# Second attention: scores of one head on 32 rows of the array, and a chunk's turns made in a step of their own

## The chip, the core and the metric

The kernel runs on one core of a Trainium2 chip. The metric is the device time of one execution in microseconds; the runs shown are three, and their median counts. The core has engines that run side by side and each work off a queue of their own in order: PE (matrix products, from SBUF into PSUM), DVE, ACT and POOL (vector work; here only the first two are given PSUM tiles, and POOL also issues indirect DMAs) and SP, which here issues DMAs. The kernel deals PSUM out in banks of 512 float32 values per partition. An engine waits for another through semaphores. PE's rows come in two kinds: PEld loads the weights (the stationary operand), PE streams the moving operand past them. A float32 matmul shows as two loads and two streams. Matmuls whose operands lie in 32 of the 128 rows, or whose outputs lie in 32 of the 128 columns, use a part of the array (32*128 or 128*32 in the rows).

## The reference

Two transformer layers over 8 sequences of 512 tokens and 256 features. Each layer normalizes, then adds an attention and a mixture of experts. The change lies in the second layer's attention, a gated linear attention with 8 heads of 32 features, which the reference writes as a scan over time:

```python
def step(M, inp):
    q_t, k_t, v_t, f_t, g_t, o_t = inp
    M = M * f_t[..., None, None] + g_t[..., None, None] * scale * (k_t[..., :, None] * v_t[..., None, :])
    y_t = jnp.einsum('bhd,bhde->bhe', q_t, M) * o_t[..., None]
    return (M, y_t)
```

`q` and `k` are rotated projections, `f`, `g` and `o` sigmoid gates by head; the rows `y` are then multiplied by `Wout` and added to the input.

## The kernel before

The scan is done by chunks of 128 tokens, `NT` = 4 per sequence. Within a chunk the sum over earlier tokens is a matrix product with a decay: for each head the scores k·q (keys on the partitions, queries along the free dimension) are multiplied by exp of the summed logs of the forget gates between the two tokens. What comes from earlier chunks goes through a state `m`, 256 by 32 values kept as two block-diagonal 128 by 128 matrices (four heads each), with decayed queries `qw` and decayed keys `kw`.

`prep1` (from L1265) makes a sequence's operands: `s_proj` (projections `pa`, `pb`, L1296, the rotation on DVE, L1311 to L1320), `s_gates`, and `s_decays` (PSUM tile `dec`, from which ACT makes `ew` and `tot`).

`main1` in `attention1` (from L1384) works through the chunks with two kinds of steps.

- `s_scores(c)`: ACT writes `u`, eight 128 by 128 tiles, one per head: the triangle `inc` times the head's logs (L1416). PE turns the chunk's queries and keys (`qkT`, L1420), ACT copies them out (L1422). Then for each half `hf` of four heads: PE puts a large negative number above the diagonal (`mask_gt`, L1426) and adds the logs' sums (`gt` times `u`, L1433) into `d`; ACT takes the exponential into `de` (L1437); DVE spreads the turned queries over four block-masked copies `qb` (L1440), so that one product over all 128 rows gives four heads' scores `a` (L1447); DVE multiplies to `am` (L1448). `d` and `a` take turns in two PSUM buffers of one bank each (pool `a1da`).
- `s_chunk(c)`: `qw` on DVE (L1460), turned on PE (L1463), copied by ACT (`qwTs`, L1465). For each half: the state's product (L1468), then four matmuls, one per head, each into its own 32 output partitions (L1472), all into `y`. ACT copies `yTs` (L1480). `kw` on DVE (L1485), its product with `v` into `pm` (L1488), from which DVE updates `m` (L1499 to L1503). Last the output product `po` (L1510) and the addition to `x` (L1513).

Eight PSUM banks are shared out as `mm` 2 (pa, pb, po), `tr` 2 (qkT, qwT), `da` 2, `y` 1, `sm` 1 (pm and dec).

`interleave` alternates the steps of sequence b with the `prep1` steps of the next. After each step `move()` issues some of a list of other steps: in part "a" (sequences 0 to 3) the end of the norms, the second layer's routing and the 64 indirect DMAs by which POOL sends rows to the experts' order (L437); in part "b" (sequences 4 to 7) the fetching (SP) and adding (DVE, L476) of the experts' results and the storing of finished sequences. Their number per step follows from `n_steps`. Between "a" and "b" the experts of layer two run, with the `prep1` of sequence 4 among them. The order in which the code issues steps is a priority: a scheduler works out a fixed order for each engine's queue before the run, and in the trace the instructions of neighbouring steps are mixed.

Of the kernel before, what the change touches and what calls it, by code (L numbers as in the profile page):

```python
# [84 lines left out]
def tile_two_layers(  # L85
# [1179 lines left out]
    def prep1(b, ap, ps_mm, ps_sm, held1, places=None):  # L1265

        wide = {"tag": "mm", "n": S} if places else {"tag": "sm", "n": 256}
# [86 lines left out]
        def s_decays():  # L1354
            flat = lf.rearrange("p t h -> p (t h)")
            ps = ps_sm.tile([P, wide["n"]], F32, tag=wide["tag"], name=f"dec{b}")
            nc.tensor.matmul(ps[:, 0:32], inc, flat, start=True, stop=True)
            nc.tensor.matmul(ps[:, 32:64], gt, flat, start=True, stop=True)

            lfx = new("lfx", NT - 2, H1, HD1)  # L1360
            nc.scalar.copy(lfx, bc(lf[:, 1 : NT - 1], HD1))
            lfx = lfx.rearrange("p t h d -> p t (h d)")
            for c in range(1, NT - 1):
                for hf in range(2):
                    n = 64 + 2 * c + hf
                    nc.tensor.matmul(
                        ps[:, n : n + 1],
                        lfx[:, c - 1, hf * P : (hf + 1) * P],
                        one,
                        start=True,  # L1370
                        stop=True,
                    )
            nc.scalar.activation(
                ew.rearrange("p i t h -> p (i t h)"), ps[:, 0:64], AF.Exp
            )
            nc.scalar.activation(
                tot[:, 1 : NT - 1].rearrange("p t i -> p (t i)"),
                ps[:, 66 : 64 + 2 * (NT - 1)],
                AF.Exp,
            )  # L1380
# [3 lines left out]
    def attention1(blocks, part, also, done, held1):  # L1384
        with tc.tile_pool(name=f"a1{part}", bufs=2) as ap, tc.tile_pool(
            name=f"a1mm{part}", bufs=2, space=PSUM
        ) as ps_mm, tc.tile_pool(name=f"a1tr{part}", bufs=2, space=PSUM) as ps_tr, tc.tile_pool(
            name=f"a1da{part}", bufs=2, space=PSUM
        ) as ps_da, tc.tile_pool(name=f"a1y{part}", bufs=1, space=PSUM) as ps_y, tc.tile_pool(
            name=f"a1sm{part}", bufs=1, space=PSUM  # L1390
        ) as ps_sm:
            wout = second["wout"]
            moves = deque(also(ap, ps_mm))
            n_steps = len(blocks) * (3 * NT + 2)
# [8 lines left out]
            def main1(b):  # L1403
# [8 lines left out]
                def s_scores(c):  # L1412

                    u = ap.tile([P, H1, P], F32, tag="u", name=f"u{b}_{c}")
                    for h in range(H1):
                        nc.scalar.activation(u[:, h, :], inc, AF.Copy, scale=lf[:, c, h : h + 1])  # L1416
# [6 lines left out]
                    am = ap.tile([P, 2, 4, P], F32, tag="am", name=f"am{b}_{c}")  # L1423
                    for hf in range(2):
                        pd = ps_da.tile([P, 4, P], F32, tag="da", name=f"d{b}_{c}_{hf}")
                        nc.tensor.matmul(  # L1426
                            pd,
                            ident_h,
                            mask_gt.unsqueeze(1).to_broadcast([P, 4, P]),
                            start=True,  # L1430
                            stop=False,
                        )
                        nc.tensor.matmul(  # L1433
                            pd, gt, u[:, 4 * hf : 4 * hf + 4, :], start=False, stop=True
                        )
                        de = ap.tile([P, 4, P], F32, tag="de", name=f"de{b}_{c}_{hf}")
                        nc.scalar.activation(de, pd, AF.Exp)  # L1437

                        qb = ap.tile([P, 4, P], F32, tag="qb", name=f"qb{b}_{c}_{hf}")
                        nc.vector.tensor_tensor(  # L1440
                            qb,
                            qkT[:, hf, :].unsqueeze(1).to_broadcast([P, 4, P]),
                            blk.unsqueeze(2).to_broadcast([P, 4, P]),
                            ALU.mult,
                        )
                        pa = ps_da.tile([P, 4, P], F32, tag="da", name=f"a{b}_{c}_{hf}")
                        nc.tensor.matmul(pa, qkT[:, 2 + hf, :], qb, start=True, stop=True)  # L1447
                        nc.vector.tensor_mul(am[:, hf], pa, de)  # L1448
                    got[c] = am

                def s_chunk(c):
                    am = got.pop(c)

                    py = ps_y.tile([P, 2, P], F32, tag="y", name=f"y{b}_{c}")
                    if c:
                        pt = ps_tr.tile([P, 4, P], F32, tag="tr", name=f"qwT{b}_{c}")
                    if c:

                        qw = ap.tile([P, H1, HD1], F32, tag="qw", name=f"qw{b}_{c}")
                        nc.vector.tensor_tensor(qw, qk[c][:, :H1], per_head(ew[:, 0, c]), ALU.mult)  # L1460
                        flat = qw.rearrange("p h d -> p (h d)")
                        for hf in range(2):
                            nc.tensor.transpose(pt[:, hf, :], flat[:, hf * P : (hf + 1) * P], ident)  # L1463
                        qwT = ap.tile([P, 2, P], F32, tag="qwT", name=f"qwTs{b}_{c}")
                        nc.scalar.copy(qwT, pt[:, :2, :])  # L1465
                    for hf in range(2):
                        if c:
                            nc.tensor.matmul(  # L1468
                                py[:, hf, :], m[:, hf, :], qwT[:, hf, :], start=True, stop=False
                            )  # L1470
                        for h in range(4):
                            nc.tensor.matmul(  # L1472
                                py[32 * h : 32 * h + 32, hf, :],
                                v[:, c, 4 * hf + h, :],
                                am[:, hf, h, :],
                                start=(c == 0),
                                stop=True,
                            )
                    yT = ap.tile([P, KD, P], F32, tag="yT", name=f"yTs{b}_{c}")
                    nc.scalar.copy(yT, py)  # L1480

                    if c < NT - 1:

                        kw = ap.tile([P, H1, HD1], F32, tag="kw", name=f"kw{b}_{c}")
                        nc.vector.tensor_tensor(kw, qk[c][:, H1:], per_head(ew[:, 1, c]), ALU.mult)  # L1485
                        pm = ps_sm.tile([P, 256], F32, tag="sm", name=f"pm{b}_{c}")
                        for hf in range(2):
# [6 lines left out]
                            )  # L1494
                        for hf in range(2):
# [20 lines left out]
                for c in range(NT):  # L1516
                    steps.append(lambda c=c: s_scores(c))
                    if c:
                        steps.append(lambda c=c: s_chunk(c - 1))
# [3 lines left out]
            def prep(b):  # L1523
                return prep1(b, ap, ps_mm, ps_sm, held1)
# [69 lines left out]
    with tc.tile_pool(name="m1w", bufs=4) as wp, tc.tile_pool(  # L1594
# [8 lines left out]
            prep1(B // 2, None, ps_p, ps_p, ready, places_of_prep()),  # L1603
# [101 lines left out]
```

## Time and profile before

| | |
|---|---|
| median of three runs | 1971.99 us (1968.79 to 1974.9) |
| the profiled execution | 1983.88 us, of which the span shown is 1982.2 |
| PE busy | 1775.9 us, 90% of the span |
| PEld busy | 1248.7 us, 63% |
| DVE, ACT, POOL busy | 825.1, 765.9, 399.2 us |
| mean granted PE clock | 0.951 |

Times in the profile are microseconds from the span's start unless marked ns. Matmuls overlap and their ends are modelled, so that a busy PE isn't PE at its peak; how long a group of matmuls really takes is read from the start of its first to the start of what follows. In a timeline row stand start, length, engine, line, operation, output<-inputs by the names in the code, the part of the array in rows*columns, the moving operand's shape and the number of instructions merged; in brackets the engine's idle time before it and what ended it. "<-issue" is time in which the profile shows nothing that was waited for.

### The profile page before, as it was taken

How to read it: one execution, taken by the hardware profiler on the slowest of the kernel's cores; microseconds unless marked ns; L12 is line 12 of the kernel's file. 1: busy time of each engine (PE TensorE's matmuls, PEld its weight loads, DVE VectorE, ACT ScalarE, POOL GpSimd, SP SyncE). 2: the span in 40 equal slices, each digit the busy share in tenths (PEclk: the TensorE clock that was granted, in tenths of full speed). 3: DMA queues.
4: the chain of work that ended last, by engine and by line, in shares of the span. 5: the costliest groups of instructions: out<-in, count | busy, mean ns of one | idle time of the engine just before them, and what ended most of it. 6: DMA issues, size and time to landing. Idle time of an engine off the chain costs nothing. (4 is left out here: it accounts for less than half of the span.)

```text
span 1982.2 us, 28295 instructions
## 1 busy us (share of the span) xinstructions
PE 1775.9 (90%) x10680; PEld 1248.7 (63%) x10680; DVE 825.1 (42%) x1886; ACT 765.9 (39%) x1432; POOL 399.2 (20%) x457
## 2 busy tenths in 40 slices
PE   5876988999999999997688469999999999999998
PEld 3434655666666666764344235578888889886455
DVE  5453333434344434344667337641111111114865
ACT  2333334344434443434345135532323333335455
POOL 2024441212212122121130660011111111011000
PEclk9988999999999999998788779999999999999999
DMA  8713220656634354333321330086666867572500
GB/s 247 196 48 141 82 92 23 192 167 179 196 120 144 132 178 135 114 112 95 113 89 35 117 119 1 1 292 218 232 227 218 309 228 262 211 298 74 165 11 22
DMA packets 163688, 289.18 MB, mean 146 GB/s; under 512 B 63952, under 2 KB 134624, under 8 KB 152928
## 3 DMA queue, kind: packets, MB, share of 16 engines
q1 hardware_dynamic: 148432, 248.77, 38.6%
q0 software_dynamic: 13088, 36.07, 4.9%
q10 hardware_dynamic: 2032, 2.54, 0.4%
q8 instruction: 84, 1.38, 0.3%
q14 instruction: 52, 0.43, 0.1%
HBM read 206.78 MB, written 67.94 MB: 139 GB/s over the span
## 5 line engine op out<-in xcount | busy, mean ns | idle before, releaser
L659 PE MATMUL gup<-xgT,ew 128*128 128x256 f32 (+1 forms) x2080 | 379.3, 337 | 3.5 <-DMA ew<-in_dram 1.9
L692 PE MATMUL gdn<-ew,hgT 128*128 128x256 f32 x1640 | 372.4, 381 | 0.0
L659 PEld LDWEIGHTS gup<-xgT,ew 128*128 128x128 f32 x2080 | 333.5, 192 | 40.3 <-issue 4.5
L692 PEld LDWEIGHTS gdn<-ew,hgT 128*128 128x128 f32 x1640 | 307.7, 190 | 48.6 <-issue 9.1
L969 DVE TENSOR_REDUCE mx<-sc 128x4 f32<-128x2048 f32 (+1 forms) x124 | 184.0, 1484 | 274.8 <-ACT pt L997 254.7
L997 ACT ACTIVATE pt<-sc 128x2048 f32<-128x2048 f32 (+3 forms) x128 | 158.3, 1237 | 238.1 <-PE sc L966 130.0
L719 POOL DMA_INDIRECT zd<-yo,row x144 | 140.1, 973 | 468.3 <-DVE yo L710 403.3
L670 ACT ACTIVATE hgT<-gup,ew 128x256 f32<-128x256 f32 (+1 forms) x376 | 133.1, 424 | 209.0 <-issue 123.2
L999 POOL TENSOR_SCALAR_AFFINE_SELECT pt<-pt 128x512 f32<-128x512 f32 x128 | 81.7, 638 | 650.1 <-ACT pt L997 648.6
L991 PE MATMUL sc<-qsh,k 32*128 32x512 f32 (+3 forms) x1024 | 114.1, 493 | 54.9 <-DVE mx L969 51.3
L710 DVE SCALAR_TENSOR_TENSOR yo<-ew,way,yo 128x256 f32<-128x256 f32 x72 | 31.7, 481 | 300.9 <-ACT yo L708 300.9
L437 POOL DMA_INDIRECT xd<-xr,pos x128 | 125.8, 983 | 61.0 <-issue 50.1
L1019 PE MATMUL av<-pt,vaug 128*32 128x512 f32 (+3 forms) x1024 | 88.6, 478 | 31.4 <-POOL pt L999 30.6
L991 PEld LDWEIGHTS sc<-qsh,k 32*128 32x128 f32 x1024 | 43.4, 187 | 113.7 <-DVE mx L969 83.8
L997 ACT ACT_TABLE_LOAD x42 | 53.9, 1283 | 158.2 <-PE sc L991 128.6
L964 PE MATMUL sc<-k,q 32*128 32x512 f32 (+1 forms) x992 | 108.1, 468 | 3.8 <-DMA k<-raw 3.8
L1019 PEld LDWEIGHTS av<-pt,vaug 128*32 128x32 f32 x1024 | 31.9, 118 | 83.1 <-issue 41.2
L1447 PE MATMUL a<-qb,qkTs 128*128 128x512 f32 x128 | 70.9, 637 | 11.9 <-DVE am L1448 9.3
L1028 DVE STREAM_TRANSPOSE ou<-av 128x512 f32<-128x512 f32 x32 | 22.9, 716 | 135.2 <-PE av L1019 119.8
L708 ACT ACTIVATE yo<-gdn,way 128x256 f32<-128x256 f32 x72 | 30.2, 473 | 125.8 <-PE gdn L692 125.7
L1433 PE MATMUL d<-u,cs 128*128 128x512 f32 x128 | 70.3, 633 | 3.9 <-ACT u L1416 3.9
L1416 ACT ACTIVATE u<-cs,lf 128x128 f32<-128x128 f32 x224 | 72.2, 394 | 0.0
(270 smaller groups left out, 2366.5 us busy)
## 6 DMA issues: line engine op xcount, KB each, us to landing
ew<-in_dram SPq DMA_DIRECT2D x47, 2180.0 KB
ew<-in_dram SPq DMA_DIRECT2D x36, 1024.0 KB
xd<-zero SPq DMA_DIRECT2D x12, 1572.0 KB
z<-zd SPq DMA_DIRECT2D x32, 512.0 KB
xnT<-in_dram SPq DMA_DIRECT2D x22, 512.0 KB
xg<-xd SPq DMA_DIRECT2D x36, 262.0 KB
xg<-xd SPq DMA_DIRECT2D x144, 64.0 KB
xn_d<-l_xn SPq DMA_DIRECT2D x16, 512.0 KB
```

What stands on the lines that cost most here:

```text
L437: i = nc.gpsimd.indirect_dma_start(out=self.xd, out_offset=bass.IndirectOffsetOnAxis(ap=self.pos[k][:, at : at + 1], axis=0), in_=held[b][ ...
L659: nc.tensor.matmul(ps[:, j, at : at + m], wu[u][:, k, f * P : (f + 1) * P], x, start=(k == 0), stop=(k == KD - 1),)
L670: nc.scalar.activation(ht[:, f, at : at + m], ps[:, j, at : at + m], AF.Gelu, bias=w[u][2][:, f : f + 1],)
L692: nc.tensor.matmul(ps[:, t, :], ht[:, f, t * P : (t + 1) * P], wd[:, f, :], start=(f == 0), stop=(f == nf - 1),)
L719: d = nc.gpsimd.indirect_dma_start(out=self.r.zd, out_offset=bass.IndirectOffsetOnAxis(ap=row[:, s : s + 1], axis=0), in_=y[:, s, :], in_o ...
L964: nc.tensor.matmul(ps[:, h, :], q[r, j * P : w], k[r, :w], start=True, stop=False)
L969: last["dve"] = nc.vector.tensor_reduce(mxs[n % 2][:, j, :, HD0], ps, AX.X, ALU.max)
L991: nc.tensor.matmul(ps[:, h, :w], k[r, i * P : (i + 1) * P], q[r, i * P :], start=True, stop=True)
L997: nc.scalar.activation(e, ps[:, :, :w], AF.Exp, scale=0.25)
L999: last["pool"] = nc.gpsimd.affine_select(out=e[:, :, :P], in_=e[:, :, :P], pattern=[[0, 4], [1, P]], base=0, channel_multiplier=-1, compar ...
L1019: nc.tensor.matmul(ps[32 * h : 32 * h + 32, i * P :], vaugs[b % 2][:, i, c : c + 32], e[:, h, :], start=(i == 0), stop=(i == NT - 1),)
L1416: nc.scalar.activation(u[:, h, :], inc, AF.Copy, scale=lf[:, c, h : h + 1])
```

## The change

The scores of a head are now computed on the 32 rows where its turned queries and keys lie, without the masked copies `qb`: eight matmuls of 32 rows and 128 columns per chunk, the four heads of a half into four different banks. They are issued ahead of the mask and the logs' sums, which go into the same four banks as columns 256 to 511. One `de` and one `am` then cover all eight heads; `u`, `de` and `am` keep the heads in another order.

A new step `s_turn(c)` holds what turns: `qkT`, the decayed queries `qw` with their turn, the decayed keys `kw`, and `u`. The steps of a sequence go turn(c), chunk(c-2), scores(c), so that a chunk's product with `v` follows its turn by two steps of its kind. In `s_chunk` `pm` comes first and shares the bank of `y`; the four heads of both halves follow one another, with the state's products before and behind them.

PSUM is shared out anew: `mm` 2, `tr` 1, `da` one buffer of four banks, `y` 1; `sm` is gone, and `dec` uses an `mm` buffer. `n_steps` grows from 14 to 18 per sequence.

```diff
         def s_decays():
             flat = lf.rearrange("p t h -> p (t h)")
-            ps = ps_sm.tile([P, wide["n"]], F32, tag=wide["tag"], name=f"dec{b}")
+            ps = ps_mm.tile([P, S], F32, tag="mm", name=f"dec{b}")
...
-        ) as ps_mm, tc.tile_pool(name=f"a1tr{part}", bufs=2, space=PSUM) as ps_tr, tc.tile_pool(
-            name=f"a1da{part}", bufs=2, space=PSUM
-        ) as ps_da, tc.tile_pool(name=f"a1y{part}", bufs=1, space=PSUM) as ps_y, tc.tile_pool(
-            name=f"a1sm{part}", bufs=1, space=PSUM
-        ) as ps_sm:
+        ) as ps_mm, tc.tile_pool(name=f"a1tr{part}", bufs=1, space=PSUM) as ps_tr, tc.tile_pool(
+            name=f"a1da{part}", bufs=1, space=PSUM
+        ) as ps_da, tc.tile_pool(name=f"a1y{part}", bufs=1, space=PSUM) as ps_y:
...
-            n_steps = len(blocks) * (3 * NT + 2)
+            n_steps = len(blocks) * (4 * NT + 2)
...
+                def s_turn(c):
+                    pt = ps_tr.tile([P, 4, P], F32, tag="tr", name=f"qkT{b}_{c}")
...
+                    if c:
+
+                        qw = ap.tile([P, H1, HD1], F32, tag="qw", name=f"qw{b}_{c}")
+                        nc.vector.tensor_tensor(qw, qk[c][:, :H1], per_head(ew[:, 0, c]), ALU.mult)
+                        flat = qw.rearrange("p h d -> p (h d)")
+                        pt = ps_tr.tile([P, 4, P], F32, tag="tr", name=f"qwT{b}_{c}")
+                        for hf in range(2):
+                            nc.tensor.transpose(pt[:, hf, :], flat[:, hf * P : (hf + 1) * P], ident)
+                        qwTs[c] = ap.tile([P, 2, P], F32, tag="qwT", name=f"qwTs{b}_{c}", bufs=3)
+                        nc.scalar.copy(qwTs[c], pt[:, :2, :])
+                    if c < NT - 1:
+
+                        kws[c] = ap.tile([P, H1, HD1], F32, tag="kw", name=f"kw{b}_{c}", bufs=3)
+                        nc.vector.tensor_tensor(
+                            kws[c], qk[c][:, H1:], per_head(ew[:, 1, c]), ALU.mult
+                        )
+
+
+                    u = ap.tile([P, 4, 2, P], F32, tag="u", name=f"u{b}_{c}")
+                    for h in range(H1):
+                        nc.scalar.activation(
+                            u[:, h % 4, h // 4, :], inc, AF.Copy, scale=lf[:, c, h : h + 1]
+                        )
+                    turns[c] = qkT, u
+
+                def s_scores(c):
+                    qkT, u = turns.pop(c)
+                    ps = ps_da.tile([P, 4, 4, P], F32, tag="da", name=f"da{b}_{c}")
                     for hf in range(2):
-                        pd = ps_da.tile([P, 4, P], F32, tag="da", name=f"d{b}_{c}_{hf}")
+                        for r in range(4):
+                            rows = slice(32 * r, 32 * r + 32)
+                            nc.tensor.matmul(
+                                ps[:, r, hf, :],
+                                qkT[rows, 2 + hf, :],
+                                qkT[rows, hf, :],
+                                start=True,
+                                stop=True,
+                            )
+                    for r in range(4):
                         nc.tensor.matmul(
-                            pd,
+                            ps[:, r, 2:, :],
                             ident_h,
-                            mask_gt.unsqueeze(1).to_broadcast([P, 4, P]),
+                            mask_gt.unsqueeze(1).to_broadcast([P, 2, P]),
                             start=True,
                             stop=False,
                         )
-                        nc.tensor.matmul(
-                            pd, gt, u[:, 4 * hf : 4 * hf + 4, :], start=False, stop=True
-                        )
-                        de = ap.tile([P, 4, P], F32, tag="de", name=f"de{b}_{c}_{hf}")
-                        nc.scalar.activation(de, pd, AF.Exp)
-
-                        qb = ap.tile([P, 4, P], F32, tag="qb", name=f"qb{b}_{c}_{hf}")
-                        nc.vector.tensor_tensor(
-                            qb,
-                            qkT[:, hf, :].unsqueeze(1).to_broadcast([P, 4, P]),
-                            blk.unsqueeze(2).to_broadcast([P, 4, P]),
-                            ALU.mult,
-                        )
-                        pa = ps_da.tile([P, 4, P], F32, tag="da", name=f"a{b}_{c}_{hf}")
-                        nc.tensor.matmul(pa, qkT[:, 2 + hf, :], qb, start=True, stop=True)
-                        nc.vector.tensor_mul(am[:, hf], pa, de)
+                        nc.tensor.matmul(ps[:, r, 2:, :], gt, u[:, r], start=False, stop=True)
+                    de = ap.tile([P, 4, 2, P], F32, tag="de", name=f"de{b}_{c}")
+                    nc.scalar.activation(de, ps[:, :, 2:, :], AF.Exp)
+                    am = ap.tile([P, 4, 2, P], F32, tag="am", name=f"am{b}_{c}")
+                    nc.vector.tensor_mul(am, ps[:, :, :2, :], de)
                     got[c] = am
...
-                    py = ps_y.tile([P, 2, P], F32, tag="y", name=f"y{b}_{c}")
...
+                    py = ps_y.tile([P, 4, P], F32, tag="y", name=f"y{b}_{c}")
                     if c < NT - 1:
...
-                        pm = ps_sm.tile([P, 256], F32, tag="sm", name=f"pm{b}_{c}")
+                        kw = kws.pop(c)
+                        pm = py[:, 2:, :].rearrange("p i t -> p (i t)")
...
+                    of_state(0)
+                    for hf in range(2):
+                        for h in range(4):
+                            nc.tensor.matmul(
+                                py[32 * h : 32 * h + 32, hf, :],
+                                v[:, c, 4 * hf + h, :],
+                                am[:, h, hf, :],
+                                start=(c == 0 or hf == 1),
+                                stop=(c == 0 or hf == 0),
+                            )
+                    of_state(1)
+                    yT = ap.tile([P, KD, P], F32, tag="yT", name=f"yTs{b}_{c}")
+                    nc.scalar.copy(yT, py[:, :2, :])
...
                 for c in range(NT):
+                    steps.append(lambda c=c: s_turn(c))
+                    if c > 1:
+                        steps.append(lambda c=c: s_chunk(c - 2))
                     steps.append(lambda c=c: s_scores(c))
-                    if c:
-                        steps.append(lambda c=c: s_chunk(c - 1))
+                steps.append(lambda: s_chunk(NT - 2))
                 steps.append(lambda: s_chunk(NT - 1))
```

## The prediction

> **What bounds the kernel now.** I read the windows view first. The change touches only the second attention, which stands in two places: part "a" from 1060 to 1290 us and part "b" from 1813 us to the end. Columns: length, busy time (and instructions) of PE, PEld, DVE, ACT and POOL, granted clock, DMA share, GB/s.
>
> ```profile
> core 0: us, PE busy (x) PEld busy (x) DVE busy (x) ACT busy (x) POOL busy (x), PEclk, DMA share, GB/s
> 1060.00:1290.00 230.00, 176.69 (x812) 98.96 (x813) 126.62 (x298) 92.52 (x241) 73.18 (x76) 0.85 0.15 52
> 1813.00:1982.20 169.20, 154.31 (x779) 87.24 (x779) 122.35 (x247) 91.56 (x238) 0.00 (x0) 0.97 0.23 75
> ```
>
> In "b" PE is busy for 154 of 169 us and the clock is nearly full; DVE has 122, ACT 92. In "a" PE has 177 of 230 and the clock is 0.85: something stops it there. The other 1583 us (L0 and both expert stages) do nothing that the diff names.
>
> Busy time of overlapping matmuls is no length, so I take lengths from start to start, in the PE timeline of "b"'s last batch, where nothing is interleaved:
>
> ```profile
> 1963.10 0.61 PE L1488 MATMUL pm<-v,kw 128*128 128x128 f32 x4
> 1963.55 0.27 PE L1420 MATMUL qkT<-cs,qk 128*128 128x128 f32 x1
> 1963.72 0.49 PE L1468 MATMUL y<-qwTs,m 128*128 128x128 f32 x2
> 1964.14 0.43 PE L1472 MATMUL y<-am,v 128*32 128x128 f32 x8
> 1964.50 0.49 PE L1468 MATMUL y<-qwTs,m 128*128 128x128 f32 x2
> 1964.91 0.43 PE L1472 MATMUL y<-am,v 128*32 128x128 f32 x8
> 1965.27 0.55 PE L1420 MATMUL qkT<-cs,qk 128*128 128x128 f32 x3
> ...
> 1966.80 1.02 PE L1433 MATMUL d<-u,cs 128*128 128x512 f32 x2
> 1967.66 1.02 PE L1447 MATMUL a<-qb,qkTs 128*128 128x512 f32 x2
> 1968.52 0.38 PE L1426 MATMUL d<-mask_gt,ident_h 128*128 128x512 bf16 x1
> 1968.73 1.02 PE L1433 MATMUL d<-u,cs 128*128 128x512 f32 x2
> 1969.59 1.07 PE L1447 MATMUL a<-qb,qkTs 128*128 128x512 f32 x2
> 1970.50 0.38 PE L1463 MATMUL qwT<-cs,qw 128*128 128x128 f32 x2
> 1970.71 0.61 PE L1488 MATMUL pm<-v,kw 128*128 128x128 f32 x4
> ```
>
> One chunk is 7.61 us from pm to pm, and no row in it names a wait: PE's own work sets the pace. A float32 matmul is two instructions. `a` takes 0.86 us (1967.66 to 1968.52), twice per chunk 1.72; `d` also 0.86; a mask 0.21. The four y rows take 1.55 (1963.72 to 1965.27).
>
> In "a" I looked for what stops PE:
>
> ```profile
> 1104.03 3.31 PE L1296 MATMUL pa<-wcat,xnT 128*128 128x512 f32 x4
> 1121.55 2.23 PE L1296 MATMUL pb<-wcat,xnT 128*128 128x280 f32 x4 [14.21 <-issue]
> ```
>
> Between about 1098 and 1190 us POOL sends 64 indirect DMAs, 1.27 us from one to the next. In three stretches of its unbroken sending DVE, ACT and PE stand still together for 4 to 15 us (pb waits for a PSUM buffer whose reader on DVE starts 16 us after its data are there). That is some 45 us that no matmul sets.
>
> **Part by part.**
>
> **Scores on 32 rows.** Out go the two `a` matmuls per chunk (1.72 us on PE) and two `qb` on DVE (0.68 each). In come eight matmuls of 32 rows and 128 columns, four heads at a time. The L0 attention already has that shape:
>
> ```profile
> 507.22 0.59 PE L659 MATMUL gup<-xgT,ew 128*128 128x256 f32 x2
> 507.75 0.93 PE L991 MATMUL sc<-qsh,k 32*128 32x384 f32 x8
> 508.50 0.40 PE L964 MATMUL sc<-k,q 32*128 32x128 f32 x8
> 508.83 0.40 PE L966 MATMUL sc<-mask_lt,ident_h 128*128 128x128 bf16 x4
> ```
>
> x8 is four heads at two instructions each. Four heads of 384 columns take 0.75 us, of 128 columns 0.33, of which the last part is the way back to the full array: (0.75 - 0.33) / 2 = 0.21 per 128 columns, so 0.11 for that way. Into it: the two gup (256 columns, 0.216 apart in this trace) would end at 507.65, sc starts at 507.75: 0.10. Two halves thus cost 0.43 + 0.21 = 0.64 us, and 1.08 us per chunk goes. The Trainium skill ("TensorE: Matmul & The Clock Gate", Part 3, measured speedup) gives 3.07x for four 32-row tiles of 512 columns: 1.72 / 3.07 = 0.56. That is for 512 columns; the row has this type and size and both switches, so 0.64 stands. By the one 37 us in all, by the other 32 x 1.08 = 34.6.
>
> **Against it** stands the skill's "TensorEngine Tiling (Array Packing)", Key Properties: a change of tiling mode drains the array. If a drain were the whole tail of a 128-column matmul (0.27 long, 0.11 to the next), a switch would cost 0.16, and 32 x 2 x 0.06 = 4 us would be lost; the rows say 0.10 and 0.11, which are in the sum already.
>
> **y in one run.** The rows above change mode four times per chunk. After, both halves' heads run together between the two state matmuls. In chunk 0, which has no state, the sixteen instructions take 0.57 us with the way back (1229.67 to 1230.24 in the PE timeline of "a"). So 0.22 (state, weights ahead) + 0.10 + 0.57 + 0.32 (state after the switch, whose second half starts 0.21 and not 0.11 later) = 1.21 against 1.55: 0.34 in the 24 chunks with state, 8.2 us.
>
> **Mask and logs' sums in four pieces of 256 columns** instead of two of 512: as many columns. Four more weight loads of 190 ns hide under 0.22 us matmuls, as gup's do; only the load after a mask (0.11) may show. From nothing to 0.08 x 4 x 32 = 10 us; in 509.06 the first matmul after a 128-column mask is late by 0.06 and a 256-column mask gives twice the cover, so I take 3 us.
>
> **ACT and DVE.** `de` once over 1024 elements: 0.60 grows by 0.43 for 512 more, 1.03 against 1.19. `am`: 0.69 grows by 0.61, 1.3 against 1.38. With `qb` gone DVE loses 1.4 us per chunk, about 46 us in all, ACT 5. Neither is the bound in the steady part, so this is worth nothing by itself; it helps where DVE is full: 1070 to 1100 (routing) and "b"'s first batch, whose x<-x,z adds cost 19.5 us. There PE's saving counts less and DVE's counts instead; about even.
>
> **Turned ahead.** `qwT`, `kw` and `u` are made a step earlier. Same work, other place: it takes away PE's wait for qwTs (2.2 us in "b", 1.9 in "a"), and `a`'s for `qb` (1.9). Of steps moved past queues: `move()` is spread over 72 steps instead of 56, so z loads and `put` on SP and the sends on POOL are handed out per shorter step; POOL sent its last at 1190, 100 us before the experts ask. `dec` now takes an `mm` buffer, which only po wants at that point: below 1 us per batch, 7 batches, hidden by up to 3 us of y and pm.
>
> **What is late next.** The score tile fills four banks and has one buffer, `tr` too, pm shares y's bank. The same page (Restrictions and Gotchas, Gotcha 1) says that row tiles must write different banks; so no double buffer is left. Before a next score PE must wait for last d, `de` 1.03, `am` 1.3 and some 0.2 of handing over: 2.5 us. What lies between on PE: transposes 0.66, pm 0.45, y 1.2, po 0.9, 3.2 us even in the last batch, 3.9 us more where projections run. Behind a waiting score stand all of PE's later instructions. Cost between 0 and 2.5 x 32 = 80 us. The near row is the present double coupling (PEld a <- DVE am: 3.7 us in "b", four handings per chunk): I take 4 us in all, which the removed waits of about 6 pay.
>
> **Sum.** 34.6 + 8.2 - 3 + 2 = 42; of it I drop 4 for chunks inside the 92 us of sending, where what is saved can run into the same standstill. So 38: the profiled execution, 1983.9 (span 1982.2 plus 1.7 around it), would be 1946. It lies 12 us over the median shown; on the median 1972 the forecast is **1934 us**. The chunk cycle above should be 7.61 - 1.08 - 0.34 = 6.2 us.
>
> **Rivals.**
> - **The single score buffer decides (slower).** At each chunk PE stops for `de` and `am`, because the order on PE, fixed before the run, puts next scores ahead of cover, or because `de` waits behind the eight `u` of the next turn (2.4 us) on ACT. From 1.2 us per chunk (38 / 32) the gain is gone; a full 2.5 us each is 80 - 42, so 2010. For: three tiles lose a buffer, and `am` grew to one long piece. Against: 3.2 us of cover; a queue order that works at four handings per chunk now. 0.12.
> - **Four heads don't overlap.** Eight times 0.22 is 1.72, plus switches 0.2: loses 6.4 where y wins 8.2: 1970. Against: the sc rows. 0.04.
> - **The sends take "a".** Gain there only outside the sending, about 13 of 21 us, and one more standstill of 10 to 15 us: 1950 to 1964. For: 45 us already lie there and more PE instructions (36 per chunk) run through it. 0.14.
> - **Gaps close as well.** "b" has gaps of over 0.2 us adding up to 15 us; should most go in both parts: 1908 to 1918. 0.10.
> - The forecast, 1918 to 1950: 0.60.
>
> What a measurement can tell from no change is 0.3%, 6 us. Faster has the last three and most of their edges, 0.82; same 0.06; slower 0.12. Leaving out two in ten, from the slower rival and the largest gain: 1912 to 1964.
>
> **What would show it.** Right: rows 32*128 32x128 on the score tile, x512, four starts close together; `a` and `qb` gone; `am` and `de` x32 at 1.3 and 1.0 us; 6.2 us from pm to pm at the end; "b" near 146 us and "a" near 210, L0 and the expert stages as they were. Wrong: a wait "<-DVE am" of over 1 us ahead of the first score in most chunks, scores starting 0.2 us apart, or longer standstills while POOL sends.

## The result, and the profile after

The changed kernel takes 1983.89 us (median of 20 runs, 1981.19 to 1992.29); the kernel before, run beside it, takes 1977.57 (20 runs). The ratio is 1.004, 95% interval 1.0024 to 1.0056: no gain, and a loss of about 0.4%. The forecast was 1934. The profiled execution of the changed kernel takes 1982.18 us, its span is 1980.4, the mean granted clock 0.942.

The windows view of the changed kernel, for the two places of the second attention (columns as before: length, busy time of PE, PEld, DVE, ACT, POOL, granted clock, DMA share, GB/s):

```profile
core 0: us, PE busy (x) PEld busy (x) DVE busy (x) ACT busy (x) POOL busy (x), PEclk, DMA share, GB/s
1060.00:1290.00 230.00, 171.51 (x1104) 118.07 (x1104) 98.75 (x244) 86.76 (x215) 73.61 (x76) 0.79 0.16 53
1813.00:1980.40 167.40, 148.86 (x1053) 103.30 (x1052) 98.38 (x194) 86.58 (x216) 0.00 (x0) 0.90 0.23 75
```

DVE does 24 to 28 us less in each part, PE and ACT some 5 to 6; the parts last as long as before. The clock column is what got worse: 0.85 to 0.79 in "a", 0.97 to 0.90 in "b".

The groups of instructions of the changed kernel in "b" (busy us and mean ns of one, then idle time of the engine before them and what ended it) show that the change does what it says:

```profile
L1448 PE MATMUL da<-qkTs 32*128 32x128 f32 x240 | 17.5, 333 | 2.4 <-ACT qkTs L1416 1.8 <-DVE am L1467 0.6
L1467 DVE TENSOR_TENSOR am<-da,de 128x1024 f32<-128x1024 f32 x16 | 19.5, 1219 | 33.9 <-ACT de L1465 33.9
L1465 ACT ACTIVATE de<-da 128x1024 f32<-128x1024 f32 x16 | 16.4, 1024 | 35.0 <-PE da L1463 34.9
```

`a` and `qb` are gone, `am` lasts 1.22 us, `de` 1.02, and the scores wait for `am` 0.6 us in all of "b". In the PE timeline of the last batch, twelve of a chunk's sixteen score instructions come in one run, and four stand ahead of `po`:

```profile
1965.03 0.49 PE L1448 MATMUL da<-qkTs 32*128 32x128 f32 x4
1965.56 1.13 PE L1525 MATMUL po<-wout,yTs 128*128 128x256 f32 x4
1966.62 0.71 PE L1448 MATMUL da<-qkTs 32*128 32x128 f32 x12
1967.27 0.28 PE L1456 MATMUL da<-mask_gt,ident_h 128*128 128x256 bf16 x1
...
1969.45 0.61 PE L1479 MATMUL y<-v,kw 128*128 128x128 f32 x4
```

The twelve start within 0.65 us of the mask behind them: four heads overlap. Added up from its columns alone (a float32 instruction of 128 columns 0.107 us, four heads at once counted once), PE's stream from a part's first `qkT` to its last addition to `x` falls from 133.6 us to 113.1 in "b" and from 133.8 to 114.5 in "a". These 20 us per part are the saving that was forecast. The length of the parts did not follow.

**Where they went** shows at a batch's end. Here is the changed kernel's timeline (PE and ACT) where the third batch of "b" ends:

```profile
1930.14 0.62 ACT L1359 COPY lfx<-lf 128x512 f32<-128x512 f32 x1 [0.26 <-DVE lf L1336]
1930.66 2.44 ACT L1437 ACTIVATE u<-cs,lf 128x128 f32<-128x128 f32 x8
...
1932.10 0.61 PE L1479 MATMUL y<-v,kw 128*128 128x128 f32 x4
...
1933.13 1.28 ACT L1465 ACT_TABLE_LOAD   x1
1933.43 0.49 PE L1491 MATMUL y<-qwTs,m 128*128 128x128 f32 x2
1933.76 0.60 PE L1414 MATMUL qkT<-cs,qk 128*128 128x128 f32 x4
1934.42 1.02 ACT L1465 ACTIVATE de<-da 128x1024 f32<-128x1024 f32 x1
1935.34 0.68 ACT L1437 ACTIVATE u<-cs,lf 128x128 f32<-128x128 f32 x2
1935.93 0.36 ACT L1507 COPY yTs<-y 128x256 f32<-128x256 f32 x1
...
1936.34 1.66 PE L1525 MATMUL po<-wout,yTs 128*128 128x256 f32 x4 [1.98 <-ACT yTs L1507]
```

The last logs' sum of chunk 3 is done at 1932.10, when `y` starts behind it. `de`, which waits for nothing else, starts at 1934.42: on ACT the eight `u` of the next batch's chunk 0 (2.44 us) stand ahead of it, then a table load. `yTs` stands behind `de` and two more `u`, though `y` was done near 1933.9. `po`, and all PE work behind it, waits 2 us. Then the clock falls, as the windows view of the same stretch shows:

```profile
core 0: us, PE busy (x) PEld busy (x) DVE busy (x) ACT busy (x) POOL busy (x), PEclk, DMA share, GB/s
1930.00:1933.40 3.40, 3.40 (x34) 2.63 (x34) 3.33 (x7) 3.24 (x10) 0.00 (x0) 1.00 0.02 5
1933.40:1936.80 3.40, 1.42 (x12) 1.12 (x9) 1.63 (x3) 3.39 (x7) 0.00 (x0) 1.00 0.00 0
1936.80:1940.20 3.40, 3.40 (x16) 3.12 (x14) 1.25 (x5) 0.85 (x3) 0.00 (x0) 0.50 0.00 0
1940.20:1943.60 3.40, 3.40 (x26) 2.30 (x26) 1.77 (x5) 1.15 (x5) 0.00 (x0) 0.50 0.00 0
1943.60:1947.00 3.40, 3.40 (x19) 2.12 (x20) 0.42 (x1) 0.37 (x1) 0.00 (x0) 0.50 0.00 0
1947.00:1950.40 3.40, 3.40 (x15) 2.30 (x12) 0.00 (x0) 0.00 (x0) 0.00 (x0) 0.50 0.45 154
```

A hole of 2 us in one window is followed by four windows (13.7 us) at half clock. PE's busy share is 100% in them, which hides that it does half the work or less. At the three batch ends of "b" PE was at half clock for 30.7 us; before the change for 10.2.

### The profile page after: what moved, and what is told of

Its sections match the earlier page's. It is cut to its first block, busy times and chain, and to the rows that moved or that the text cites. A ratio compares the mean times of both kernels' runs of the same rounds, so it can differ in the third digit from the quotient of the medians.

```text
span 1980.4 us, 29258 instructions
## 1 busy us (share of the span) xinstructions
PE 1759.7 (89%) x11256; PEld 1280.6 (65%) x11256; DVE 778.9 (39%) x1790; ACT 761.3 (38%) x1400; POOL 397.5 (20%) x457
## 5 line engine op out<-in xcount | busy, mean ns | idle before, releaser
L1463 PE MATMUL da<-u,cs 128*128 128x256 f32 x256 | 77.7, 405 | 0.2 <-ACT u L1437 0.2
L1467 DVE TENSOR_TENSOR am<-da,de 128x1024 f32<-128x1024 f32 x32 | 39.1, 1222 | 92.6 <-ACT de L1465 70.9
```

The costliest lines, as they stand in the source:

```text
L1463: nc.tensor.matmul(ps[:, r, 2:, :], gt, u[:, r], start=False, stop=True)
```

## The experiments

The first theory (A): ACT's order at a batch's end makes PE wait, and the low clock behind the wait costs more than the wait. Rivals: the single `tr` and `da` buffers (B); the row-tiled matmuls themselves hold the clock down (C); turning ahead is what loses, and the rows alone would gain (D). Runs of one group shared a chip and the runs of before; the groups landed on chips that differ, in part "a" above all. So the ratio is always to before on the same chip, and part "b" (first `qkT` to last addition to `x`, from one profiled execution each), which lasts 169.7 and 169.8 us in the two profiles of the kernel before, on different chips, is the yardstick across groups. "Half clock" is the time in it at a granted clock of 0.5. Part "a", where it is given, runs from its first projection (`pa`) to its last addition.

| run | before, us | ratio (95% interval) | part b, us | half clock, us |
|---|---|---|---|---|
| kernel before / changed, first chip | 1977.6 | 1.004 (1.0024 to 1.0056) | 169.7 / 170.5 | 10.2 / 30.7 |
| e1_act_order | 1915.6 | 0.9867 (0.9849 to 0.9885) | 162.1 | 20.5 |
| e2_rows_only | 1915.6 | 1.001 (0.9999 to 1.002) | 170.9 | 30.7 |
| e3_ahead_only | 1915.6 | 0.9992 (0.9983 to 1.0001) | 168.6 | 6.8 |
| e4_pe_filled | 1915.6 | 0.9891 (0.9876 to 0.9906) | 163.1 | 10.2 |
| c_after | 1918.4 | 1.0005 (0.9996 to 1.0014) | 169.7 | 30.7 |
| c_before | 1918.4 | 1.0011 (0.9998 to 1.0024) | 169.8 | 10.2 |
| e5_order_and_fill | 1918.4 | 0.9846 (0.9832 to 0.9859) | 157.1 | 10.2 |
| e6_pe_refilled | 1918.4 | 1.0067 (1.0052 to 1.0083) | 175.4 | 10.2 |
| e7_rows_order | 1972.1 | 1.0065 (1.0047 to 1.0084) | 175.6 | 37.5 |
| e8_before_order | 1972.1 | 0.9984 (0.9969 to 1.0) | 170.0 | 10.2 |
| e9_ahead_order | 1972.1 | 0.9992 (0.9978 to 1.0007) | 167.1 | 3.4 |
| e10_before_order_fill | 1972.1 | 0.9981 (0.9964 to 0.9997) | 170.8 | 10.2 |
| e11_part_filled | 1974.7 | 0.9971 (0.9952 to 0.999) | 162.6 | 13.7 |
| c_e1 | 1974.7 | 0.9947 (0.9927 to 0.9966) | 160.5 | 17.1 |
| c_e5 | 1974.7 | 0.9931 (0.9906 to 0.9956) | 156.4 | 3.4 |

**e1: ACT's order alone.** PE's and DVE's queues are those of the changed kernel, instruction for instruction; only ACT's differs.

```diff
-                    for h in range(H1):
-                        nc.scalar.activation(
-                            u[:, h % 4, h // 4, :], inc, AF.Copy, scale=lf[:, c, h : h + 1]
-                        )
+                    with behind(*(("de", "yT") if c == 0 else ())):
+                        for h in range(H1):
+                            nc.scalar.activation(
+                                u[:, h % 4, h // 4, :], inc, AF.Copy, scale=lf[:, c, h : h + 1]
+                            )
...
-                    nc.scalar.activation(de, ps[:, :, 2:, :], AF.Exp)
+                    last["de"] = nc.scalar.activation(de, ps[:, :, 2:, :], AF.Exp)
...
-                    nc.scalar.copy(yT, py[:, :2, :])
+                    copied = nc.scalar.copy(yT, py[:, :2, :])
+                    if c == NT - 2:
+                        last["yT"] = copied
```

> The changed kernel with one thing else: at the end of each batch the eight u of the next batch's chunk 0 stand on ACT behind de of chunk 3 and the yT copy of chunk 2; PE's and DVE's orders are those of the changed kernel. Theory A (ACT's order at a batch's end makes PE wait 2.1 us for yTs at six places, and each wait is followed by 7 to 14 us at half clock): the waits po<-yTs fall below 1 us, the half-clock stretch behind them goes, part b falls from 167 to about 145-152 us, the whole kernel comes to 1945-1960 us, ratio to the kernel before 0.983-0.992. Rival (the boundary waits are only two of many; the single tr and da buffers cost the gain): 2 us off each of six boundaries and nothing more, 1968-1976 us, ratio 0.996-1.000. Rival (the gaps only move: PE then waits for the next batch's u or qkT instead): 1980-1986 us, ratio 1.002-1.006.

A gain of 1.3%, where the changed kernel stands at 1.0005 on such a chip. The second batch's end of "b" in e1's timeline:

```profile
1808.65 1.02 ACT L1466 ACTIVATE de<-da 128x1024 f32<-128x1024 f32 x1
1809.57 0.37 ACT L1508 COPY yTs<-y 128x256 f32<-128x256 f32 x1
...
1809.98 1.13 PE L1528 MATMUL po<-wout,yTs 128*128 128x256 f32 x4 [0.62 <-ACT yTs L1508]
```

`yTs` follows `de` at once and PE's wait is 0.62 us instead of 1.98. Theory A holds in sign and in the whole time, and the rival "two of many waits" is out by far. But part "b" came only to 162.1, not to 145-152, and half clock still is 20.5 us: the rest of the wait (a table load of 1.28 us ahead of `de`) still drops it. Nor are there six such places: at the first batch end of "b" no `u` stands ahead of `de`, the table load stands between `de` and `yTs`, and PE's wait of 1.32 us there is the same with and without the edit.

Most of the gain lies in "a", where all three batch ends have the wait (1.98 us each in c_after, 0.62 in e1). Here is that part, on chips without the standstill described below, in the kernel before (c_before), the changed kernel (c_after) and e1 (columns as before):

```profile
1007.00:1219.00 212.00, 190.96 (x935) 106.91 (x934) 150.21 (x357) 109.62 (x271) 84.83 (x79) 0.98 0.21 69
1009.00:1226.50 217.50, 191.78 (x1223) 127.67 (x1222) 126.69 (x309) 107.22 (x255) 84.09 (x79) 0.91 0.21 68
1006.70:1207.80 201.10, 179.23 (x1222) 118.49 (x1221) 123.06 (x308) 107.20 (x255) 83.60 (x79) 0.97 0.22 73
```

The time at half clock in them is 10.2, 41.0 and 13.7 us.

**e2 and e3: one half of the change each.** e2 keeps the scores on 32 rows in the old order of steps; e3 turns ahead with the scores as before.

```diff
-                    steps.append(lambda c=c: s_turn(c))
-                    if c > 1:
-                        steps.append(lambda c=c: s_chunk(c - 2))
                     steps.append(lambda c=c: s_scores(c))
-                steps.append(lambda: s_chunk(NT - 2))
+                    if c:
+                        steps.append(lambda c=c: s_chunk(c - 1))
```

That is e2 against the changed kernel; the turns of `qkT` and `u` go back into `s_scores`, those of `qw` and `kw` into `s_chunk`. e3 against the kernel before:

```diff
+                    steps.append(lambda c=c: s_turn(c))
+                    if c > 1:
+                        steps.append(lambda c=c: s_chunk(c - 2))
                     steps.append(lambda c=c: s_scores(c))
-                    if c:
-                        steps.append(lambda c=c: s_chunk(c - 1))
+                steps.append(lambda: s_chunk(NT - 2))
```

> The scores on 32 rows with the step order of before: nothing is turned two steps ahead, each chunk's queries and keys are turned in its own scores step and the decayed ones in its own chunk step. Theory A and the theory that the turning ahead is what loses: the 2.1-us waits for yTs at batch ends shrink, and the kernel lies below the kernel before by 10 to 30 us (ratio 0.985-0.995). Theory C (row-tiled matmuls and the loss of double buffers in tr and da are what loses): it is no faster than the changed kernel, 1983 us or more, with a wait for qwTs or qkTs in each chunk; ratio 1.003-1.03.

> The turning two steps ahead alone: scores as before, a whole-array matmul against block-masked queries (qb), PSUM buffers as before. Theory A: the order of ACT at the batch ends is the same as in the changed kernel, so the 2-us waits for yTs and long half-clock stretches are there, and without the scores' saving the kernel is slower than before by 5 to 25 us (ratio 1.003-1.013). Theory C (it is the row-tiled matmuls that keep the clock at half): the half-clock stretches stay as short as before (10 us in all of part b), and it is 2 to 6 us faster than before from the removed waits for qwTs (ratio 0.997-0.999).

Neither moves the time. For e2 the waits of PE in "b" (total us, times, longest) say why:

```profile
engine line waited for: us in total, times, longest us
PE y L1493 <- ACT qwTs L1434: 16.3, 6, 5.1
PE da L1450 <- ACT qkTs L1416: 3.4, 2, 2.7
PE po L1527 <- ACT yTs L1509: 2.0, 5, 0.5
```

Without the turning ahead, PE stands up to 5.1 us for the decayed queries' copy; D falls. e3 has neither the long waits nor the low clock; its ACT order turned out better than the expectation assumed (only five `u` between the two halves of `de`), so it says nothing against A, and its short half clock alone can't be put down to the missing row tiles (C; the last section takes it up).

**e4 and e11: fill PE, leave the wait.** The filling writes into `po`'s own bank, which `po` then overwrites: e4 ten times in every batch (2.1 us), e11 four times (0.86 us) in batches with a batch behind them.

```diff
                     po = ps_mm.tile([P, S], F32, tag="mm", name=f"po{b}_{c}")
+                    if c == NT - 2 and b != blocks[-1]:
+                        for _ in range(4):
+                            nc.tensor.matmul(
+                                po,
+                                ident_h,
+                                mask_gt.unsqueeze(1).to_broadcast([P, 4, P]),
+                                start=True,
+                                stop=True,
+                            )
```

> The changed kernel with ten bf16 matmuls of 512 columns (2.1 us, into po's own bank, overwritten by the po that follows) ahead of po of chunk 2 in every batch, so that PE does not stand still while it waits for yTs. Theory A: the wait stays but the clock does not fall; the half-clock stretches at batch ends vanish, 5 to 7 us come back at each of six boundaries, less up to 2 us in the two batches without a boundary; ratio to before 0.985-0.993. Rival (the clock is not what costs; the wait is): the time does not change or grows by up to 6 us, ratio 1.004-1.010.

> The changed kernel with only four bf16 matmuls of 512 columns (0.86 us) ahead of po of chunk 2 in the six batches with a batch behind them; ACT's order is the changed kernel's, so PE still stands for some 1.2 us there. If the clock is set by the share of a 3.41-us window in which PE streams (half when it is below about 0.4, back at full only from about 0.75): the half-clock stretches at the batch ends of part b go though the wait stays, and part b falls to 163 us or less, as in e4 (163.1). If a stop of over 1 us is itself what halves the clock: the stretches stay and part b is 168-171 us.

e4 adds 80 useless matmuls, makes no `yTs` come earlier, and gains 1.1%. e11 is the sharper of the two. Its timeline where the second batch of "b" ends:

```profile
1885.17 1.03 PE L1526 MATMUL po<-mask_gt,ident_h 128*128 128x512 bf16 x4
1885.84 1.02 ACT L1465 ACTIVATE de<-da 128x1024 f32<-128x1024 f32 x1
1886.76 0.68 ACT L1437 ACTIVATE u<-cs,lf 128x128 f32<-128x128 f32 x2
1887.34 0.36 ACT L1507 COPY yTs<-y 128x256 f32<-128x256 f32 x1
...
1887.75 1.13 PE L1534 MATMUL po<-wout,yTs 128*128 128x256 f32 x4 [1.55 <-ACT yTs L1507]
```

And the windows view of the same kernel from there on:

```profile
1886.00:1889.00 3.00, 1.45 (x9) 1.15 (x8) 2.11 (x6) 3.00 (x9) 0.00 (x0) 1.00 0.00 0
1889.00:1892.00 3.00, 2.92 (x36) 2.36 (x35) 1.96 (x7) 1.21 (x6) 0.00 (x0) 1.00 0.00 0
1892.00:1895.00 3.00, 3.00 (x10) 1.89 (x11) 0.76 (x3) 0.50 (x1) 0.00 (x0) 1.00 0.16 57
```

PE still waits 1.55 us there, and the clock stays at 1.00 behind it: in the clock's window of 3.41 us around the wait PE streams for 0.44 of the time (how this share is counted stands in the last section). At the third end the same wait of 1.55 us falls into a window with a share of 0.34, and the clock does drop. So a stop of over 1 us is not by itself what halves it. At the first and third ends a stretch of 6.8 us is left, where the changed kernel has 10.2 and 13.7. Although `yTs` comes no earlier, part "b" is 162.6: nearly all that e1 gains by bringing it forward. So the clock, not the wait, is the larger part. In the whole time e11 gains 0.3%, and e1 on the same chip 0.5% (c_e1); their "a" (267.6 and 261.7 us) has the standstills told of next in it.

**c_after and c_before: the two kernels on the chip of e5 and e6.**

> The changed kernel itself, beside the kernel before on the chip of this job. The six experiments' ratios so far came from a chip on which the kernel before takes 1916 us, not 1978. If the loss at batch ends is a matter of ACT's order and of the clock, it is there on any chip: ratio 0.998-1.006, with 2.1-us waits for yTs and half-clock stretches of 7 to 14 us at the batch ends of part b. If it came from the sends of part a on the other chip, the ratio here is below 0.992.

> The kernel before, unchanged, for its profile on the chip of this job: ratio 1.000 by construction, part b 168-170 us with two half-clock stretches of 3 to 7 us, part a shorter than the 270 us of the first chip if a shorter standstill in the sends is what makes the chips differ.

Part "b" lasts as long as on the first chip, low clock and all; part "a" is 217.4 us in c_after, not 271.1. What differs is a standstill while POOL sends, here in the windows view of the changed kernel on the first chip:

```profile
1097.00:1127.00 30.00, 3.84 (x23) 2.78 (x24) 3.77 (x7) 2.22 (x4) 18.92 (x22) 0.50 0.32 109
```

The same view of c_after, over nearly all of its sending:

```profile
1085.00:1160.00 75.00, 70.90 (x462) 49.87 (x461) 42.94 (x91) 38.27 (x95) 59.09 (x62) 0.86 0.43 140
```

PE has gaps of more than 3 us between starts in "a" that add up to 43 us (before) and 33 (changed) on the first chip, and none on this one, with the same 64 sends, most of them 1.27 us apart on both. Why one chip stops there was not tried. It accounts for most of the 60 us between the medians of before ("a" 269.2 and 211.7), and not for the change's missing gain.

**e5: the order, and four fillings** (e1's and e11's edits together).

> ACT's order of e1 and, in the six batches with a batch behind them, four bf16 matmuls of 512 columns (0.86 us) ahead of po of chunk 2, as long as the wait of 0.8 us that e1 has left there. If a window of 3.41 us in which PE streams for less than 0.4 of the time is what halves the clock for the next one or two, the stretches of 3.4 to 6.8 us that e1 still shows at its batch ends go: 3 to 10 us below e1, ratio 0.981-0.986. If e1's leftover half clock comes from elsewhere: as e1 or up to 3 us slower, ratio 0.986-0.989.

The best version: 1888.31 us against 1918.35, within the first of the two ranges. Its part "b" is 157.1 us, its "a" 197.4 (before 211.7). At the first batch end of "b" a stretch of 6.8 us at half clock stays.

**e6: the saved work put back.** Ten bf16 matmuls of 256 columns per chunk behind the scores, overwritten by the mask.

```diff
+                    for i in range(10):
+                        nc.tensor.matmul(
+                            ps[:, i % 4, 2:, :],
+                            ident_h,
+                            mask_gt.unsqueeze(1).to_broadcast([P, 2, P]),
+                            start=True,
+                            stop=True,
+                        )
                     for r in range(4):
```

> The changed kernel with the time saved in the scores put back as useless work on PE: ten bf16 matmuls of 256 columns (1.07 us) behind the scores of every chunk, into a bank that the mask overwrites; ACT's order at the batch ends is the changed kernel's. If PE's own work still sets the pace, 32 x 1.07 = 34 us are added: ratio to before 1.015-1.022. If the saved time had become waiting, and waiting at half clock (theory A with the clock as the larger part), the filling costs next to nothing or even gains: ratio 0.995-1.006.

Between the two: 34 us more on PE lengthen the kernel by about 12 (1931.13 against 1919.61). So some two thirds of what was put back fell into time in which PE stood or was kept from running at half clock. Half clock falls from 30.7 us to 10.2, although ACT's order is the changed kernel's at two of the three batch ends of "b": there PE waits 1.2 us, in windows with a share of 0.43, and the clock stays full.

**e7, e8, e9, e10: whose gain is the order?** e1's edit on e2, on the kernel before and on e3; e10 is e8 with e11's filling.

> The scores on 32 rows without the turning ahead (as e2), with e1's order on ACT at a batch's end. If rows and order make the gain and turning ahead adds little: ratio 0.985-0.991, near e1's 0.987. If turning ahead is needed (without it PE waits in each chunk for qwTs, which is copied behind the scores' de): ratio 0.995-1.002, near e2's 1.001.

> The kernel before with e1's order on ACT at a batch's end, nothing else. There the second de of chunk 3 already stands ahead of the eight u, and only two or five u stand ahead of yTs. If the gain of e1 belongs to the change (which put the eight u ahead): ratio 0.998-1.002. If the order is a gain of its own, whatever the scores: ratio 0.985-0.993.

> The turning ahead without the scores on 32 rows (as e3), with e1's order on ACT at a batch's end. If rows make the gain: ratio 0.996-1.000, as e3 (0.9992) or a little below. If turning ahead with the right order makes it: ratio below 0.993.

> e8 with e5's four bf16 matmuls (0.86 us) ahead of po of chunk 2 in the six batches with a batch behind them. If keeping PE's windows filled is worth as much in the kernel before as in the changed one: ratio 0.990-0.997. If the kernel before has no such hole there, since its PE has a fuller stream (131 us of 163 in part b, against 111): six times 0.86 us are added or hidden, ratio 0.999-1.004.

All four with the same rule for ACT, part "b": kernel before 170.0, rows alone 175.6, turning ahead alone 167.1, both 162.1 (c_e1 160.5). The two halves of the change need each other: rows alone lose about 6 us in "b", as the waits for `qwTs` are 14.4 us and half clock rises to 37.5; together they gain 8 to 10. e7 missed both ranges, being slower than either said. e8 and e10 are 0.2% faster than before (e10 lies between its two ranges), with no gain in "b": the order's worth belongs to the change, which is what put the `u` ahead.

**c_e1 and c_e5: the versions on a chip like the first.**

> e1 again: part b 160-164 us whatever the chip. On a chip where before takes about 1972 us the ratio is 0.985-0.995; on one with 1916 us 0.986-0.989.

> e5 again: part b 156-159 us whatever the chip. On a chip where before takes about 1972 us the ratio is 0.982-0.993; on one with 1916 us 0.983-0.986.

Part "b" is as on the other chip. The ratios are nearer to 1 (c_e5 just misses its range), because part "a" with its standstills gives less: 260.7 us in c_e5 against 269.2 in the kernel before on the first chip.

## Why the prediction was wrong

- **Right:** four heads overlap; `am` and `de` at about 1.3 and 1.0 us (1.22, 1.02); PE's stream about 20 us shorter in each part; the single score buffer costs almost nothing (0.6 us of waits for `am` in "b"; no run put two row tiles into one bank); L0 and the experts stay (their stretches differ by 1 to 3 us between the profiles).
- **The step that failed is "Turned ahead": "Same work, other place", booked as a gain of waits.** The place was the error. On PE it is a gain: e2 shows 16.3 us of waits for `qwTs` when it is taken back. But `u` goes along, and at a batch's end the next batch's eight `u` came to stand on ACT ahead of this batch's last `de` and `yTs`. The text saw "`de` waits behind the eight `u` of the next turn (2.4 us) on ACT", but only in a rival's clause, for each chunk and through the score buffer. It happens at batch ends only (five of the six), and through `yTs` and `po`: PE waits 1.98 us at each in c_after. Freeing the order (e1) brings 1.3% on the chip without standstills, and 0.5% (c_e1) on one with them.
- **The sum took PE's stream for time and had no term for the clock.** Each saved microsecond also empties a window. The half clock at batch ends tripled (10.2 to 30.7 us in "b"), which is up to 10 us of work lost, and e11 wins back 8 us of "b" by filling alone. The rival "Gaps close as well" had the sign wrong: PE's gaps of over 0.2 us in "b" went from 11.4 us to 16.4, and the clock fell behind them.
- **Steady chunks: 6.2 us was right for one step of the last batch only.** From one addition to `x` to the next it is 7.33 and then 6.23, against 7.54 both times before. In the PE waits of the changed kernel in "b" the single `tr` buffer shows:

```profile
PE po L1525 <- ACT yTs L1507: 6.5, 6, 2.0
PE y L1479 <- DVE kw L1430: 2.6, 1, 2.6
PE qwT L1424 <- ACT qkTs L1416: 2.4, 4, 0.7
```

  `qwT` waits until `qkT` has been copied out of the one buffer. This is theory B: 2.4 us in "b", real but small.
- **What is left of the sum.** For "b" 21 us were forecast (half of 42); e5 and c_e5 get 13 (169.8 to 157.1, 169.7 to 156.4). So 13 of the 21 lay in the order and the clock. One part of the other 8 can be read off. Sixteen score instructions in one run take 0.66 us up to the mask (0.64 was forecast), but in 9 of the 16 chunks of "b" (7 in e5) other matmuls stand among them, and two runs of 6 and 10 take 0.53 and 0.64: 0.5 us more each time, some 3.5 us in e5's "b". The rest was not settled one by one; waits for `kw`, `qkTs`, `qk` and `z` add up to some 8 us in e5's "b", but the kernel before has waits of its own. In "a", without the standstills, e5 gets 14 of the 20.

## What to carry to other kernels

When work is moved to an earlier step, list for every engine, and above all at the seam between two loops' bodies, what it will stand ahead of in that queue; a helper of the next batch ahead of the last copy of this one costs more than its length. When PE's stream is cut and a gap stays, count the stream in the window around the gap: the saving itself can bring the clock down. A few useless matmuls in the gap are a cheap test of that, and here they were part of the best version (0.9846 and 0.9931 of before on the two chips).

## What the runs showed of the hardware

**The clock has two thresholds.** In all 17 profiles the granted clock changes on a grid of 3.41 us. For each window of that grid I took the share of it in which PE streams (columns as above, twice as long at half clock; the matmuls with 8 rows or 8 columns, which run one at a time, count in full), and looked at the clock of the window behind it. These are all 9540 windows:

```text
clock now   share of the window   next at half   next at full
full        0.43 and more                    2           8262
full        0.25 to 0.43                   154             97
full        below 0.25                     189              0
half        below 0.65                     447              0
half        0.65 to 0.78                    61             24
half        0.78 and more                    0            304
```

At full speed a share of 0.43 or more was followed by half twice in 8264 windows, and one below 0.25 always; at half speed it took some 0.65 to 0.78 to come back. Between the limits the share, as it can be counted here, doesn't decide. In the changed kernel at 1933.38 the share is 0.29; the windows behind have 0.40, 0.58, 0.70 and 1.01 of half speed, and only after the last does the clock return. Before the change the stretches were shorter, with shares of 0.59, 1.00 and 0.86. The Trainium skill ("TensorE: Matmul & The Clock Gate", Part 1) has the window of 3413 ns and warns of idle gaps longer than that; by it a wait of 2 us would cost 2 us. In this trace four windows at half speed followed it, up to 6.8 us more. The measurement decides: a gap well under a window is enough if what surrounds it is thin.

Theory C, that row tiles count for less in this share, does not fit these traces. The table counts four tiles of 32 rows at once as one full stream. Counted so, the best single limit leaves 29 windows at full clock on the wrong side and 20 at half clock; with row tiles at half that weight it is 61 and 74, at double 83 and 75.

**Chips gave one kernel times 60 us apart** (1972 to 1978 in three of the groups above, 1916 to 1918 in two), nearly all of it in part "a", where POOL sends. A gain measured on one chip alone would have been put at 1.5% or at 0.7% (e5 and c_e5).
